# Corner weights by columns on ScalarE in a four-layer convolution network: three buffers, and two pauses in the order

## The chip, the cores and the metric

The kernel runs on one NeuronCore of one Trainium2 chip. A core has five engines with queues of their own, and each executes its queue strictly in order: TensorE (PE in the profile, with its weight loads as PEld), VectorE (DVE), ScalarE (ACT), GpSimd (POOL) and SyncE (SP), which here only starts DMAs. GpSimd starts DMAs too: the indirect gathers. The metric is the device time of one execution in microseconds (us). The kernel before takes 7763.29 us, the median of 8 runs that lie between 7756.68 and 7767.76.

## The reference

The input is four images of 256 channels and 64 x 64 pixels, all in float32. Four layers follow, each `x = x + layer(groupnorm(x))`:

- **Layer 0, deformable convolution.** A 1x1 convolution with batch norm and leaky ReLU gives `y`. A projection of `y` is the picture that is sampled. A 3x3 depthwise convolution of `y` gives, for each pixel, 4 groups and 9 points, an offset and a softmax weight. Each point is sampled bilinearly, so from four corners with four weights, and the 9 points of a group are summed:

```python
return tap(x0, y0, (1 - wx) * (1 - wy)) + tap(x0 + 1, y0, wx * (1 - wy)) \
     + tap(x0, y0 + 1, (1 - wx) * wy) + tap(x0 + 1, y0 + 1, wx * wy)
...
dout = (samp * mr).sum(-1)
```

  Then come an output projection, a squeeze-and-excite scaling by channel means over the whole image, and a feedforward 256 to 1024 to 256.
- **Layer 1, linear attention.** A 1x1 convolution gives q, k, v; a 5x5 depthwise convolution gives a second set; heads of 8 channels compute `vk = v k^T`, `out = vk q / (sum(k) q + eps)`, then a projection.
- **Layer 2, a 3x3 convolution** with binarised weights.
- **Layer 3, attention against pooled keys**: 4096 queries, 1024 keys from a 2x2 max pool, softmax, output convolution.

## The kernel before, in words

**The sampling.** For each image a table in DRAM holds, for each pixel, a row of 256 numbers: the 64 channels of one group at that pixel and its neighbours, so that one gathered row has all four corners of a point. `sample` (from line 557) walks an image in 16 blocks (NBLK) of 18 rounds (BR), 288 rounds in all. In each round `gathered` (L589) starts four indirect gathers from GpSimd's queue, one per group, each of 128 rows into a tile `g` (seven buffers). The row numbers are read from the tile `sl`, which a DMA fills for each block. TensorE then does eight small matmuls (L602): the gathered rows against a matrix `wm` of 128 rows and 16 columns for each corner, which holds the row's corner weight in the column of the pixel that the row belongs to and zero elsewhere. So the matmul weighs the corners and sums the points at once, into `acc`.

**The matrices `wm`.** `weigh` (L582) makes them for three rounds (WR) at a time: an array of 128 x (3 rounds x 16 corners x 16 columns). One VectorE instruction multiplies the table `own` (which column a row belongs to, the same for all) with the 48 weights of the three rounds. There are two buffers. The product for the next three rounds is called in the first round of the present three.

**What follows `acc`.** Each two rounds ScalarE copies `acc` to SBUF (`moved`, L607), TensorE transposes it (`turned`, L612), ScalarE copies the result in two halves into `dT` (`spread`, L622). After a block come the output projection (L635), two additions and a batch norm.

**The other work beside it.** The sampling of image n runs with other images' later layers beside it, all in one order written by the program: `beside` (in `run`) advances the sampling by one round and then each other generator until its spent cost matches its share. The totals that these shares are of are constants: FEED for the feedforward, LINEAR for the linear attention, SECOND for layer 2 and 3 of an image. The first image's convolution runs ahead; then come four stages: image 0's sampling beside the other images' convolutions and offsets; image 1's beside binarising, image 0's feedforward (the first fifth) and linear attention (the rest); images 2 and 3 beside the feedforward and linear attention of the image before and, from 0.2 to 0.9 of the stage, layers 2 and 3 of the one before that. After the last gather the rest of the images' layers run. In these stages TensorE, VectorE, ScalarE and GpSimd execute in the very order in which the program lists the instructions.

**The linear attention's output** (`output`, L911). For half a row block (1024 pixels): `dens` makes the denominators on TensorE (L919), `inverse` adds eps and takes the reciprocal on VectorE (L923, L924), `head` spreads the reciprocals over the channels with TensorE (`rden`, L932), `scaled` multiplies on VectorE (`ot`, L936), `proj` projects (L941), `relu` is ScalarE's (L945). They stand in a list; `staged` lines them up in steps, and each step of the generator takes one from the list. The depthwise 5x5 convolutions (L178, 25 instructions a chunk on VectorE, about 1.3 us each) run between.

**The pooled attention** (`layer3`). For 128 queries at a time: scores (L1185), maximum (L1186), exponential on ScalarE (`pe`, L1191), transposes (L1197), a copy on ScalarE (`pT`, L1199), the values (L1203), the reciprocal of the sum (L1206) and the scaling on ScalarE (`m`, L1208). After four of these the output convolution reads `m` on TensorE (L1212) and the result is added. A `yield` with a cost stands between these pieces, and is where other work is let in.

Of the kernel before, what the change touches and what calls it, by code (L numbers as in the profile page):

```python
# [9 lines left out]
F32 = mybir.dt.float32  # L10
I32 = mybir.dt.int32
AF = mybir.ActivationFunctionType
ALU = mybir.AluOpType
# [4 lines left out]
P = 128  # L18
# [3 lines left out]
NB = HW // 512  # L22
NT = HW // P
G, PT = 4, 9
# [5 lines left out]
RP, WR, UR, BG = 14, 3, 2, 2  # L30
RS, GP = RP * PT, RP * PT + 2
BR, BP, OB = PT * BG, GP * BG, RP + 2
NBLK = HW // BP
# [5 lines left out]

CONVOLVE, OFFSETS, BINARY = NB * 9 + 26, 60, 62  # L40
FEED = NB * 40 + 8
LINEAR, LAST, ASIDE = 930, 592, 9
STEPS = 900
CONV, SECOND = NB * 22.5 + 11, 555
EPS_BN = 1e-5
EPS_GN = 1e-5
EPS_ATT = 1e-5
# [24 lines left out]
class Net:  # L72
# [485 lines left out]
    def sample(self, n, ssum):  # L558

        nc, sp = self.nc, self.sp
        table = self.tab[n].rearrange("g y x s c -> (g y x) (s c)")
        blocks, images, at, dp, dT, po, later = {}, {}, {}, {}, {}, {}, {}

        def halves(name):

            t = self.ps1.tile([P, 2, 256], F32, name=name, tag=name)
            return cycle([t[:, 0], t[:, 1]])  # L570

        accs, dps = halves("acc"), halves("dp")

        def load(b):
            blocks[b] = sl = sp.tile([P, BR, G * 5], F32, name="sl")
            for h in range(BG):
                rows = self.s_d[n][(b * BG + h) * GP * PT:(b * BG + h + 1) * GP * PT]
                to = sl[:, h * PT:(h + 1) * PT]
                nc.sync.dma_start(to[0:RS], rows[0:RS * PT].rearrange("(r p) f -> p r f", p=RS))
                nc.sync.dma_start(to[RS:P], rows[RS * PT:].rearrange("(p r) f -> p r f", r=PT))  # L580

        def weigh(b, r):  # L582

            wm = self.gp.tile([P, WR, 4 * G, OB], F32, name="wm")
            sh = [P, WR, 4 * G, OB]
            nc.vector.tensor_tensor(  # L586
                wm, self.con("own").unsqueeze(1).unsqueeze(1).to_broadcast(sh),
                blocks[b][:, r:r + WR, G:].unsqueeze(3).to_broadcast(sh), ALU.mult)
            return wm  # L589

        def gathered(sl, wm, acc, r):
            r4, acc = r % WR, acc[:, r % UR * P:(r % UR + 1) * P]
            g = self.gp.tile([P, G, 256], F32, name="g", bufs=7)
            for i in range(G):
                nc.gpsimd.indirect_dma_start(  # L595
                    out=g[:, i, :], out_offset=None, in_=table,
                    in_offset=bass.IndirectOffsetOnAxis(ap=sl.bitcast(I32)[:, r, i:i + 1], axis=0))


            for x in range(2):  # L600
                for i in range(G):
                    nc.tensor.matmul(acc[32 * i:32 * i + 32, :], wm[:, r4, 4 * i + 2 * x:4 * i + 2 * x + 2, :],  # L602
                                     g[:, i, x * P:(x + 1) * P], start=x == 0, stop=x == 1)

        def moved(acc, u):
            at[u] = sp.tile([P, UR, P], F32, name="at")
            nc.scalar.copy(at[u].rearrange("p v c -> p (v c)"), acc)  # L607

        def turned(u):
            dp[u] = next(dps).rearrange("p (v g s o) -> p v g s o", v=UR, g=G, s=2)  # L610
            for v in range(UR):
                nc.tensor.transpose(dp[u][:, v].rearrange("p g s o -> p (g s o)"), at[u][:, v], self.ident)  # L612

        def spread(b, r, u):

            if b not in dT:
                dT[b] = sp.tile([P, G, BR, OB], F32, name="dT", bufs=1)
                images[b] = sp.tile([P, KT, BP], F32, name="yb")
                nc.sync.dma_start(images[b], self.y_d[n][:, :, b * BP:(b + 1) * BP])
            for s in range(2):  # L620
                hs = slice(64 * s, 64 * s + 64)
                nc.scalar.copy(dT[b][hs, :, r:r + UR], dp[u][hs, :, :, s, :].rearrange("p v g o -> p g v o"))  # L622

        def shared(b):


            v = dT[b].rearrange("p g (h r) o -> p (g h) o r", r=PT)
            both = sp.tile([P, G * BG, 2], F32, name="both")
            nc.vector.tensor_reduce(both, v[:, :, RP:], AX.X, ALU.add)
            nc.scalar.copy(v[:, :, RP:, 0], both)  # L630

        def project(b, m):
            po[m] = self.ps("po")
            for k in range(G):
                nc.tensor.matmul(po[m][:, 0:BR * OB], self.ow[:, k, m * P:(m + 1) * P], dT[b][:, k].rearrange("p r o -> p (r o)"), start=k == 0, stop=k == G - 1)  # L635

        def add(b, m):
            ym = images[b][:, m].rearrange("p (h q) -> p h q", h=BG)
            pm = po[m][:, 0:BR * OB].rearrange("p (h r o) -> p h r o", h=BG, o=OB)
            y4 = ym[:, :, 0:RS].rearrange("p h (r o) -> p h r o", o=RP)  # L640
            nc.vector.tensor_tensor(y4, pm[:, :, :, 0:RP], y4, ALU.add)
            nc.vector.tensor_tensor(ym[:, :, RS:], pm[:, :, 0, RP:], ym[:, :, RS:], ALU.add)

        def finish(b, m):
            ym = images[b][:, m]
            nc.scalar.activation(ym, ym, AF.Identity, bias=self.sh[:, 4 + m:5 + m],
                                 scale=self.inv[:, 4 + m:5 + m], accum_out=ssum[:, m, b:b + 1])
            if m == KT - 1:
                nc.sync.dma_start(self.x2_d[n][:, :, b * BP:(b + 1) * BP], images[b])

        load(0)
        wm = weigh(0, 0)
        for i in range(NBLK * BR):
            b, r = divmod(i, BR)
            for f in later.pop(i, ()):
                f()
            if r % UR == 0:
                acc = next(accs)
            gathered(blocks[b], wm, acc, r)
            if r == 0 and b + 1 < NBLK:  # L660
                load(b + 1)
            if r % WR == 0 and (r + WR < BR or b + 1 < NBLK):
                nxt = weigh(*divmod(i + WR, BR))
            if r % UR == UR - 1:
                todo = [partial(moved, acc, i), partial(turned, i), partial(spread, b, r + 1 - UR, i)]

                todo = [(i + 1 + j + (j == 2 and r < UR) * (6 - 3), f) for j, f in enumerate(todo)]
                if r == BR - 1:
                    todo += [(i + 3, partial(shared, b))]
                    todo += [(i + 6 + m + j, partial(f, b, m)) for m in range(KT) for j, f in enumerate((project, add, finish))]  # L670
                for j, f in todo:
                    later.setdefault(j, []).append(f)
            if r % WR == WR - 1:
                wm = nxt
            yield 1
        for i in sorted(later):
            for f in later[i]:
                f()
# [73 lines left out]
    def layer1(self, n, st, st2):  # L752
        nc, tc, a = self.nc, self.tc, self.a
        rw = lambda v: v.rearrange("p (r w) -> p r w", w=W)
        fl = lambda v: v.rearrange("p r w -> p (r w)")
        with tc.tile_pool(name=f"la{n}", bufs=1, side="right") as sp, \
# [3 lines left out]
            pw = sp.tile([P, 4, C], F32, name="pw")  # L760
# [3 lines left out]
            nc.vector.tensor_tensor(qb, qb, self.vec("qkv_s", n=6), ALU.mult)  # L764
            nc.vector.tensor_tensor(qb, qb, self.vec("qkv_b", n=6), ALU.add)
            yield 6
            ln = sp.tile([P, 4, P], F32, name="ln")
            ld = sp.tile([P, 4, 2, 32], F32, name="ld")
            nc.vector.memset(ld, 0.0)

# [122 lines left out]

            def summed(t):

                pc = self.ps("comb").rearrange("p (e o) -> p e o", e=2)
                for kind in range(2):
                    j = 2 * kind + t
                    nc.vector.tensor_tensor(ln[:, j], sums[:, t, kind], self.con("bd"), ALU.mult)
                    kk = sp.tile([P, 1], F32, name=f"kk{j}")  # L900
                    nc.vector.tensor_reduce(kk, ks[t][:, kind, 0:(NB, NCH)[kind]], AX.X, ALU.add)
                    for h in range(2):
                        nc.vector.tensor_scalar(ld[:, j, h, 16 * h:16 * h + 16], self.con("oh"), kk, None, ALU.mult)
                for kind in range(2):
                    nc.tensor.matmul(pc[:, kind], ln[:, 2 * kind + t], pw[:, 2 * kind + t], start=True, stop=True)
                    nc.vector.tensor_copy(pw[:, 2 * kind + t], pc[:, kind])

            def output(c, qp, aq):
# [47 lines left out]
                none = ()  # L956
# [2 lines left out]
                    staged([(dens, inverse), none, none] + order + [none, outs[1, 0], outs[1, 1]])  # L959
                else:  # L960
                    joined = lambda *fs: [f() for f in fs]
                    items = [(partial(joined, dens, inverse),)]
                    for h in range(2):
                        items += [(partial(joined, *heads[h, j]),) for j in range(4)]
                        items += [(partial(joined, *outs[h, m][:2]), outs[h, m][2]) for m in range(KT)]
# [134 lines left out]
    def layer3(self, n, st, wide=False):  # L1100
        nc, tc, a = self.nc, self.tc, self.a
        M = HW // 4
        with tc.tile_pool(name=f"na{n}", bufs=1, side="left") as sp, \
# [69 lines left out]
            for b in range(NB):  # L1173
                m2 = bp.tile([P, 512], F32, name="m2")
                for j in range(4):
# [30 lines left out]
                    nc.vector.reciprocal(rden, ps[:, P:P + 1])  # L1206
                    yield 1.5
                    nc.scalar.activation(m2[:, j * P:(j + 1) * P], ps[:, 0:P], AF.Copy, scale=rden)  # L1208
                r = self.block(bp, self.x5_d[n], b, "r5", bufs=1)
                for k in range(KT):  # L1210
                    ps = self.ps()
# [171 lines left out]
```

## Time and profile before

| what | value |
|---|---|
| median of 8 runs | 7763.29 us (7756.68 to 7767.76) |
| the profiled execution: its time, its span | 7755.36 us, 7753.6 us |
| first and last gather start | 132.6 us, 6266.0 us |
| TensorE, VectorE, GpSimd, ScalarE busy | 76%, 66%, 66%, 28% of the span |
| gathers | 4608, mean 976 ns, median 946 ns |
| wm products on VectorE | 384, mean 953 ns |

A group on the page names line, engine, operation, the tile written and those read, how often, then the busy time with the mean of one, and last the idle time of the engine just before these instructions with what ended most of it. "issue" means that the profile shows nothing waited for. A line of the waits has the waiting engine and line, what released it, the total in us, how often, and the longest. A line of the timeline has its start, its length, the engine and the instruction, with the idle time before it in brackets. Engines count as busy while an instruction runs on them; instructions of ScalarE in a row overlap a little.

### The profile page before, as it was taken

To read this page: it belongs to the slowest core of one execution; us is meant where nothing else is said; L and a number is where in the kernel's file an instruction comes from. 1 tells how busy PE (TensorE), PEld (TensorE's weight loads), DVE (VectorE), ACT (ScalarE), POOL (GpSimd) and SP (SyncE) were. 2 spreads that over 40 slices of the span, in tenths; PEclk is the share of its full clock that TensorE was granted. 3 is DMA by queue.
4 is the path that set the end of the run, shared out by engine and by line. 5 is a ranking of instruction groups with operands and counts; after the bars stand their busy time and mean duration, and the time that the engine had idled before them with its cause. 6 is when DMAs were issued, how large, how long until landed. Compare 5 with 4: busy or idle time off the path is not lost. (4 is left out here: it accounts for less than half of the span.)

```text
span 7753.6 us, 94114 instructions
## 1 busy us (share of the span) xinstructions
PE 5927.1 (76%) x35776; PEld 3477.8 (45%) x35776; DVE 5117.7 (66%) x6404; ACT 2170.5 (28%) x4648; POOL 5091.1 (66%) x4894
## 2 busy tenths in 40 slices
PE   5666666579676677889767778987677789967899
PEld 2333333334333333346544433465454435744487
DVE  6555553644788887239888882288888834999523
ACT  1111111212222211222233222222332223666315
POOL 2777777777777777777677667677776621977210
PEclk7676776779777677999888888998888889978899
DMA  6564665555544444555544455465444432211221
GB/s 188 151 179 137 172 173 140 170 176 157 159 125 122 127 139 132 167 152 161 149 138 134 121 153 166 138 166 152 142 133 124 126 123 77 65 49 38 69 80 52
DMA packets 744340, 1031.41 MB, mean 133 GB/s; under 512 B 354128, under 2 KB 459984, under 8 KB 742352
## 3 DMA queue, kind: packets, MB, share of 16 engines
q0 software_dynamic: 221184, 604.27, 27.1%
q1 hardware_dynamic: 522704, 421.10, 18.3%
q8 instruction: 284, 4.65, 0.2%
q14 instruction: 168, 1.38, 0.1%
HBM read 856.39 MB, written 168.61 MB: 132 GB/s over the span
## 5 line engine op out<-in xcount | busy, mean ns | idle before, releaser
L595 POOL DMA_INDIRECT g<-tab,sl x4608 | 4497.7, 976 | 1767.9 <-issue 1270.4
L178 DVE SCALAR_TENSOR_TENSOR agg<-pad,vec,agg 128x1024 f32<-128x1024 f32 x2257 | 2904.8, 1287 | 61.8
L602 PE MATMUL acc<-g,wm 128*32 128x128 f32 x18432 | 1298.8, 324 | 1208.6 <-ACT at L607 683.0
L602 PEld LDWEIGHTS acc<-g,wm 128*32 128x32 f32 x18432 | 636.2, 122 | 1921.9 <-ACT at L607 896.1
L1085 PE MATMUL ps<-xd,w 128*128 128x256 f32 x3072 | 716.4, 385 | 4.0 <-ACT v L828 1.7
L586 DVE TENSOR_TENSOR wm<-con,sl 128x768 f32<-128x768 f32 x384 | 365.9, 953 | 422.6 <-PE acc L602 409.1
L1085 PEld LDWEIGHTS ps<-xd,w 128*128 128x128 f32 x3072 | 578.2, 193 | 105.6 <-issue 26.7
L622 ACT COPY dT<-dp 64x128 f32<-64x128 f32 x1152 | 296.8, 258 | 1124.6 <-PE dp L612 790.7
L734 PE MATMUL ps<-x2f,f 128*128 128x512 f32 x1024 | 479.3, 616 | 4.0 <-ACT f L709 4.0
L820 PE MATMUL ps<-xr,qw 128*128 128x512 f32 x768 | 451.8, 719 | 18.3 <-DVE ot L936 7.7
L744 PE MATMUL ps<-hm,f 128*128 128x512 f32 x1024 | 462.0, 599 | 0.0
L719 DVE SCALAR_TENSOR_TENSOR hm<-ps,vec,lk 128x512 f32<-128x512 f32 x256 | 192.1, 751 | 399.3 <-ACT lk L736 394.3
L200 POOL TENSOR_TENSOR av<-av,m 128x1024 f32<-128x1024 f32 x144 | 344.1, 2389 | 105.5 <-ACT m L196 96.8
L1036 POOL TENSOR_TENSOR xd<-xp 128x640 f32<-128x640 f32 x64 | 79.4, 1270 | 492.7 <-DMA xp<-x 266.4
L607 ACT COPY at<-acc 128x256 f32<-128x256 f32 x576 | 214.3, 372 | 519.4 <-PE acc L602 507.8
L736 ACT ACTIVATE lk<-ps,low 128x512 f32<-128x512 f32 x256 | 175.9, 687 | 595.2 <-PE ps L734 595.2
L635 PE MATMUL po<-dT,ow 128*128 128x288 f32 x1024 | 310.7, 453 | 21.6 <-ACT dT L630 14.8
L1203 PE MATMUL ps<-gt,pT 128*128 128x129 f32 x2048 | 303.8, 308 | 29.4 <-ACT pT L1199 29.0
L1203 PEld LDWEIGHTS ps<-gt,pT 128*128 128x128 f32 x2048 | 287.7, 220 | 74.1 <-ACT pT L1199 42.0
L612 PE MATMUL dp<-ident,at 128*128 128x128 f32 x1152 | 273.3, 325 | 60.0 <-ACT dT L622 47.9
L734 PEld LDWEIGHTS ps<-x2f,f 128*128 128x128 f32 x1024 | 191.2, 194 | 230.6 <-issue 217.8
L874 ACT COPY kt<-pt 128x512 f32<-128x512 f32 x256 | 149.3, 584 | 501.0 <-PE pt L870 500.8
(243 smaller groups left out, 7542.4 us busy)
## 6 DMA issues: line engine op xcount, KB each, us to landing
g<-tab,sl POOLq DMA_INDIRECT x4608
x<-x SPq DMA_DIRECT2D x128, 512.0 KB
xr<-x SPq DMA_DIRECT2D x96, 512.0 KB
tab<-xo SPq DMA_DIRECT2D x192, 128.0 KB
x<-in_x SPq DMA_DIRECT2D x32, 512.0 KB
y<-yc SPq DMA_DIRECT2D x32, 512.0 KB
yb<-y SPq DMA_DIRECT2D x64, 256.0 KB
x<-yb SPq DMA_DIRECT2D x64, 256.0 KB
```

The lines of the kernel that those rows point to most:

```text
L178: nc.vector.scalar_tensor_tensor(to, s, wt, acc, ALU.mult, ALU.add)
L200: nc.gpsimd.tensor_tensor(acc, acc, made[t - 1], ALU.add)
L586: nc.vector.tensor_tensor(wm, self.con("own").unsqueeze(1).unsqueeze(1).to_broadcast(sh), blocks[b][:, r:r + WR, G:].unsqueeze(3).to_broad ...
L595: nc.gpsimd.indirect_dma_start(out=g[:, i, :], out_offset=None, in_=table, in_offset=bass.IndirectOffsetOnAxis(ap=sl.bitcast(I32)[:, r, i: ...
L602: nc.tensor.matmul(acc[32 * i:32 * i + 32, :], wm[:, r4, 4 * i + 2 * x:4 * i + 2 * x + 2, :], g[:, i, x * P:(x + 1) * P], start=x == 0, st ...
L622: nc.scalar.copy(dT[b][hs, :, r:r + UR], dp[u][hs, :, :, s, :].rearrange("p v g o -> p g v o"))
L635: nc.tensor.matmul(po[m][:, 0:BR * OB], self.ow[:, k, m * P:(m + 1) * P], dT[b][:, k].rearrange("p r o -> p (r o)"), start=k == 0, stop=k ...
L734: nc.tensor.matmul(ps, f1[:, k, m * P:(m + 1) * P], x2[:, k], start=k == 0, stop=k == KT - 1)
L744: nc.tensor.matmul(ps, f2[:, k, m * P:(m + 1) * P], hm[:, k], start=k == 0, stop=k == 4 * KT - 1)
L820: nc.tensor.matmul(ps, qw[:, k, m * P:(m + 1) * P], x[:, k], start=k == 0, stop=k == KT - 1)
L1085: nc.tensor.matmul(ps[:, e], w[:, k, t, 2 * half + e, m * P:(m + 1) * P], v[:, 2 * half + e, k, t:t + 8], start=i % 6 == 0, stop=i % 6 == 5)
L1203: nc.tensor.matmul(ps[:, 0:P + 1], pT[:, m], gt[:, m], start=m == 0, stop=m == 7)
```

## The change

`weigh` now returns the tile and a function `columns`, which writes the sixteen columns of `wm` one by one on ScalarE: the 48 weights times one column of `own`, given as the scale of an activation. The tile has three buffers instead of two. The columns of the three rounds after next are written in the second and third round of the present three, eight in each; those of the first six rounds of an image are written at its start. VectorE's product is gone.

Two pauses are added: an empty item behind the reciprocals in the list of the linear attention's output (in the stages with sampling; the last image's list had such items already), and a `yield 1.5` behind the fourth scaling of the pooled attention. The totals LINEAR and SECOND are raised with them. The tile `ln` of the linear attention, four parts kept for an image, becomes a rotating one of two parts.

```diff
-LINEAR, LAST, ASIDE = 930, 592, 9
+LINEAR, LAST, ASIDE = 938, 592, 9
-CONV, SECOND = NB * 22.5 + 11, 555
+CONV, SECOND = NB * 22.5 + 11, 568
...
-            wm = self.gp.tile([P, WR, 4 * G, OB], F32, name="wm")
-            sh = [P, WR, 4 * G, OB]
-            nc.vector.tensor_tensor(
-                wm, self.con("own").unsqueeze(1).unsqueeze(1).to_broadcast(sh),
-                blocks[b][:, r:r + WR, G:].unsqueeze(3).to_broadcast(sh), ALU.mult)
-            return wm
+            wm = self.gp.tile([P, WR, 4 * G, OB], F32, name="wm", bufs=3)
+
+            def columns(o0, o1):
+                for o in range(o0, o1):
+                    nc.scalar.activation(wm[:, :, :, o], blocks[b][:, r:r + WR, G:], AF.Copy, scale=self.con("own")[:, o:o + 1])
+
+            return wm, columns
...
-        wm = weigh(0, 0)
+        weights = [weigh(0, r) for r in range(0, 2 * WR, WR)]
+        for _, columns in weights:
+            columns(0, OB)
...
-            gathered(blocks[b], wm, acc, r)
+            gathered(blocks[b], weights[0][0], acc, r)
             if r == 0 and b + 1 < NBLK:
                 load(b + 1)
-            if r % WR == 0 and (r + WR < BR or b + 1 < NBLK):
-                nxt = weigh(*divmod(i + WR, BR))
+            if r % WR and i - r % WR + 2 * WR < NBLK * BR:
+                if r % WR == 1:
+                    weights.append(weigh(*divmod(i - 1 + 2 * WR, BR)))
+                weights[2][1]((r % WR - 1) * OB // 2, r % WR * OB // 2)
...
-            ln = sp.tile([P, 4, P], F32, name="ln")
...
+                ln = bp.tile([P, 2, P], F32, name="ln", tag="v1")
...
-                    items = [(partial(joined, dens, inverse),)]
+                    items = [(partial(joined, dens, inverse),), none]
...
                     nc.scalar.activation(m2[:, j * P:(j + 1) * P], ps[:, 0:P], AF.Copy, scale=rden)
+                yield 1.5
                 r = self.block(bp, self.x5_d[n], b, "r5", bufs=1)
```

More of the change, by code (lines that the diff above doesn't have):

```diff
@@ L673, in sample @@
             if r % WR == WR - 1:
-                wm = nxt
+                weights.pop(0)
             yield 1
@@ L898, in summed @@
                     j = 2 * kind + t
-                    nc.vector.tensor_tensor(ln[:, j], sums[:, t, kind], self.con("bd"), ALU.mult)
+                    nc.vector.tensor_tensor(ln[:, kind], sums[:, t, kind], self.con("bd"), ALU.mult)
                     kk = sp.tile([P, 1], F32, name=f"kk{j}")
@@ L904, in summed @@
                 for kind in range(2):
-                    nc.tensor.matmul(pc[:, kind], ln[:, 2 * kind + t], pw[:, 2 * kind + t], start=True, stop=True)
+                    nc.tensor.matmul(pc[:, kind], ln[:, kind], pw[:, 2 * kind + t], start=True, stop=True)
                     nc.vector.tensor_copy(pw[:, 2 * kind + t], pc[:, kind])
```

## The prediction

> **What bounds the kernel now.** I read the page's totals first.
>
> ```profile
> span 7753.6 us, 94114 instructions
> ...
> PE 5927.1 (76%) x35776; PEld 3477.8 (45%) x35776; DVE 5117.7 (66%) x6404; ACT 2170.5 (28%) x4648; POOL 5091.1 (66%) x4894
> ```
>
> No engine is full, so the stages must be read one by one. The windows between the first gathers of the four images and the end of the last one (columns: window, length, then busy time of PE, weight loads, DVE, ACT, POOL, granted clock, DMA share):
>
> ```profile
> 132.00:1622.00 1490.00, 963.83 (x6596) 501.20 (x6596) 801.26 (x1115) 253.63 (x693) 1129.93 (x1152) 0.70 0.57 162
> 1623.00:3118.00 1495.00, 1103.32 (x6660) 550.07 (x6661) 1057.35 (x1121) 331.43 (x840) 1128.37 (x1152) 0.77 0.49 142
> 3118.00:4692.00 1574.00, 1249.51 (x8481) 759.54 (x8480) 1140.69 (x1377) 444.27 (x1039) 1118.67 (x1153) 0.89 0.50 147
> 4692.00:6267.00 1575.00, 1251.06 (x8482) 760.62 (x8481) 1140.71 (x1377) 444.38 (x1039) 1119.98 (x1153) 0.89 0.50 144
> ```
>
> 6134 of the 7754 us are gathering, 1152 gathers to a stage. The groups on the page say what a gather costs.
>
> ```profile
> L595 POOL DMA_INDIRECT g<-tab,sl x4608 | 4497.7, 976 | 1767.9 <-issue 1270.4
> ...
> L586 DVE TENSOR_TENSOR wm<-con,sl 128x768 f32<-128x768 f32 x384 | 365.9, 953 | 422.6 <-PE acc L602 409.1
> ```
>
> The mean is 976 ns, the median of the line 946, and 0.30 us passes between two undisturbed gathers: 1.25 us, or 1440 us for 1152. The stages take 1490, 1495, 1574 and 1575 us. So POOL sets the end of each, and there are 374 us over the floor: gathers longer than 946 ns (30 x 4608 = 138 us) and longer pauses before them. The timeline shows what a long gather lies beside.
>
> ```profile
> 3015.69 0.95 POOL L595 DMA_INDIRECT g<-tab,sl  x1 [0.30 <-issue]
> ...
> 3016.44 0.95 DVE L586 TENSOR_TENSOR wm<-con,sl 128x768 f32<-128x768 f32 x1
> 3016.95 1.27 POOL L595 DMA_INDIRECT g<-tab,sl  x1 [0.31 <-issue]
> ...
> 3018.52 0.94 POOL L595 DMA_INDIRECT g<-tab,sl  x1 [0.30 <-DMA g<-tab,sl]
> ```
>
> The gather that starts while VectorE multiplies two SBUF operands takes 1.27 us instead of 0.95. Laid over each other for the whole trace, 354 gathers took over 1.0 us; 234 of them overlap one of the 384 wm products, and hold 104 of the 138 us (28, 27, 25 and 24 by stage). The scalar_tensor_tensor of L178 with one large SBUF operand lies beside many more gathers and leaves them at 0.95.
>
> The pauses come from the waits of POOL in the third stage; the fourth is alike, while the first two have 12.2 and 19.4 us on the second of these lines.
>
> ```profile
> POOL g L595 <- issue: 309.2, 1014, 0.6
> POOL g L595 <- PE acc L602: 121.8, 65, 7.1
> ```
>
> POOL waits for TensorE to free a gather buffer. Without the usual 0.30 us that is 121.8 - 65 x 0.30 = 102 us. Some 19 of them (23.2 us in 13 waits) lie in the feedforward at 3280 to 3510, where TensorE is full:
>
> ```profile
> 3280.00:3510.00 230.00, 209.02 (x1180) 106.22 (x1173) 73.35 (x139) 62.33 (x142) 160.07 (x164) 0.96 0.52 151
> ```
>
> The other 83 lie where both attentions run; from 4350 to 4600 alone 56.1 us in 19 waits, with VectorE busy 214 of 250 us and TensorE 195.
>
> **The change, part by part.** *The product leaves VectorE.* 384 x 953 ns = 366 us of VectorE go, and its waits for TensorE before them (409 us; 32 in the third stage, most in the first two, where VectorE has room). VectorE itself sets no stage, so this is worth what POOL gets of it. First the long gathers: in stages one and two POOL hardly waits, and 28 + 27 us come off; in the other two some of a shorter gather is spent in the next wait, and I take three quarters of 49, 37. Together -92. Bounds 0 and -104.
>
> On this the Trainium skill speaks against the change: "SBUF — State Buffer", Who interferes with whom, says that a product of two SBUF inputs takes only the read half of the port pair shared with GpSimd, and infers that descriptor generation, which writes, isn't held up by it. By that this term would be nothing. The 234 long gathers say otherwise here; the same section also has that a GpSimd instruction that reads SBUF is held up, and this one reads its row numbers there.
>
> *The waits of POOL for TensorE.* In 4350 to 4600, VectorE loses 14 products of 0.953 us and 1.6 us of waits, 15 us. That is 30% of the 50.4 us of stall there (56.1 - 19 x 0.30). The two pauses take away TensorE's waits in that window for the pooled attention's scaled rows (ACT m L1208, 8.9 us) and for the reciprocal (DVE rd L924, 5.6 us): 14.5 us or 29%. What they let pass meanwhile is the next round's work on the same queue. The two overlap, and not each microsecond reaches POOL: I take 45% of 83, 37 us for each of stages three and four, -75. Bounds 0 and -166. The feedforward's 19 us stay, as TensorE is full, and so do the few in the first two stages.
>
> *ScalarE's columns.* 384 x 16 = 6144 activations of 48 elements, in eights, in two of three rounds. The nearest rows with a scale from a column, both operands in SBUF, and one narrow strided copy:
>
> ```profile
> L630 ACT COPY dT<-both 128x16 f32<-128x16 f32 x64 | 13.1, 205 | 223.9 <-DVE both L629 223.9
> L709 ACT ACTIVATE f<-f,ex 128x1024 f32<-128x1024 f32 x8 | 8.7, 1141 | 0.0
> L1133 ACT ACTIVATE gw<-gw,g_r 128x128 f32<-128x128 f32 x8 | 2.9, 393 | 0.2 <-PE ps L1124 0.2
> ```
>
> From 1024 to 128 elements is 0.835 ns an element, so 48 take 393 - 80 x 0.835 = 326 ns. Two of L1213 (807 ns each) end within 1.51 us, so neighbours overlap by 0.10: 0.226 us apart, 1.9 us for eight, 1389 us in all, 347 a stage. The ends are 0.105 apart (the copy of 16 less the overlap; 645 us) and 0.326 (no overlap; 2003 us). I take 0.226, as the same form with the same operands gives it. ScalarE then has 444 + 347 = 791 of 1574 us in stages three and four, from 28% to 50%, and at the upper end 61%: not the bound on its own. The cover is that it waits. In the third stage it waited 145 us for the feedforward's sums, 135 and 105 us for transposes, and the columns, due four rounds later, stand ahead of those waits on its queue. The third buffer was last read by matmuls that the copy of acc before them has waited for already.
>
> What stays is that a copy behind a burst is up to 1.9 us later. TensorE's waits for ScalarE other than the copy of acc were 53 us in the third stage (m 15, pe 15, dT 13, smaller ones 10). Grown with ScalarE's load (x 1.8) they add 43, of which POOL feels about a third to a half, since it stood 102 us while TensorE was idle 324: +20 a stage, +40. Bounds 0 and +86; beyond that it is the rival below.
>
> *Starts.* Each image begins with 32 columns (7.3 us) where one product stood. Seven gather buffers, 7 x 5 us, cover it: 0, or +7 each if the buffers were full. In the built program VectorE now has chunk work ahead of the first image's last coordinates, since no wm product bars its queue: at most 5 x 1.29 + 1.33 + 4 x 0.63 = 10 us before the first gather, and SP issues one 512 KB load earlier. Part is covered by the table's writes: +4, ends 0 and +10.
>
> *The rest.* LINEAR and SECOND only follow the lengthened lists (one more step per output, 1.5 per block). The linear layer's ln in a rotating buffer waits for a free one twice an image: 0. After the last gather the pauses only reorder image 2's attention: 0, within 8 either way; the last image runs alone, where a pause is none.
>
> Sum: -92 - 75 + 40 + 4 = -123. The profiled execution took 7755.4 us (span 7753.6 and 1.8 around it), so 7632. It lies 7.9 under the median of the runs shown, below the lowest of them; on the median I expect 7640.
>
> **Rivals.** *All waits go.* VectorE at 86% in the attention windows speaks for it, the full TensorE in the feedforward against: -104, -166 and some +10 give 7503.
> *The port alone.* TensorE is 79% busy in stages three and four and could keep POOL waiting whatever VectorE does: 7763 - 92 + 44 = 7715.
> *The product does not hold up a gather*, the skill's rule told above; worked out from the rows, the long gathers then stay and come from something beside the products: 7763 - 75 + 44 = 7732. The line 0.95, 1.27, 0.94 is against it.
> *Slower: ScalarE's bursts on TensorE's path.* A round in the attentions goes from TensorE to ScalarE and back (pe, pT, kt, at) within 5 us; a burst ahead of one of them holds TensorE and so the buffers. Stages three and four have 2 x 192 bursts of 1.9 us. Without the +40 the change gains 163, so it turns at 163 / 384 = 0.42 us of a burst on the path. At 0.6 us it gives 7763 - 163 + 230 = 7830. For it: ScalarE is often blocked in order (m waits 68 us for VectorE in the third stage) and then catches up with nearly twice the work. Against: it is idle 72% of that stage.
>
> **How the numbers follow.** Forecast 0.40, its own spread 7570 to 7690; all waits 0.12; port alone 0.23; no port 0.07; slower 0.15; an even balance 0.03. 0.2% is 16 us, about what a measurement of this kernel can tell from no change. The two small gains can shrink into that, so faster 0.80, same 0.05, slower 0.15. The range from 7500 takes in nearly all of the first rival and ends at 7770, where the slower case begins; about 0.18 is left out.
>
> **What would show it.** Right: wm on ScalarE x6144 near 326 ns; ScalarE busy near 3560 us, VectorE near 4750; the gather's mean near 953; stages near 1462, 1468, and 1538 twice; POOL's waits for acc from 277 to about 200. The port step is wrong if the mean stays at 976, the second if stages three and four stay above 1550 with short gathers. The forecast fails if TensorE's waits for pe, pT, kt and dT grow by more than they lose.

## The result and the profile after

The changed kernel takes 7736.64 us (median of 11 runs, 7730.67 to 7740.28) against 7761.06 for the kernel before in the runs taken with it: a ratio of 0.9969, 95% interval 0.9961 to 0.9976. It is 24 us or 0.31% faster; 123 us were forecast, and the range began at 7500 and ended at 7770. So the sign and the range held, and the size was five times too large. The profiled execution took 7733.04 us, with a span of 7731.3.

The windows between the first gathers of the images (columns as before: window, length, busy time of PE, PEld, DVE, ACT, POOL, clock, DMA share, GB/s):

```profile
138.00:1604.00 1466.00, 955.47 (x6598) 498.48 (x6598) 715.77 (x1025) 606.48 (x2262) 1108.78 (x1152) 0.70 0.57 164
1604.00:3072.00 1468.00, 1091.44 (x6667) 547.64 (x6668) 966.86 (x1009) 674.66 (x2342) 1101.10 (x1152) 0.78 0.49 145
3072.00:4655.00 1583.00, 1253.97 (x8480) 760.23 (x8478) 1059.07 (x1281) 792.71 (x2575) 1097.84 (x1152) 0.89 0.50 146
4655.00:6239.00 1584.00, 1257.58 (x8493) 762.14 (x8481) 1059.80 (x1282) 792.88 (x2575) 1098.69 (x1152) 0.89 0.49 143
```

The first two stages came down from 1490 and 1495 us to 1466 and 1468, as forecast (1462 and 1468). The third and fourth were to fall to 1538 and rose from 1574 and 1575 to 1583 and 1584. The groups on the page and, below them, the waits of POOL in the third stage:

```profile
L596 POOL DMA_INDIRECT g<-tab,sl x4608 | 4406.4, 956 | 1831.3 <-issue 1266.7
...
L588 ACT ACTIVATE wm<-sl,con 128x48 f32<-128x48 f32 x6144 | 1487.0, 364 | 24.8 <-DMA sl<-sd 11.7
```

```profile
POOL g L596 <- issue: 305.0, 1000, 0.6
POOL g L596 <- PE acc L603: 159.6, 84, 6.6
```

The gather's mean fell from 976 to 956 ns, which is 20 x 4608 = 92 us. That is the size of the port term, though not by its working: a mean of 953 ns or 104 us was looked for, of which 92 were to reach the stages. But POOL's waits for TensorE in the third stage, less the usual 0.30 us of each, rose from 102 to 159.6 - 84 x 0.30 = 134 us, where they were to fall to 65 or, with ScalarE's price, 85. The first gather starts at 138.3 us instead of 132.6, and what follows the last gather takes 1492 us instead of 1487. Together: -24 - 28 + 9 + 10 + 6 + 5 = -22, the difference of the spans.

What TensorE waited for in the third stage, in the kernel before:

```profile
PE acc L602 <- ACT at L607: 189.1, 86, 12.1
PE ps L1212 <- ACT m L1208: 14.9, 6, 5.8
PE pt L1197 <- ACT pe L1191: 14.9, 11, 4.3
...
PE rden L932 <- DVE rd L924: 6.0, 3, 4.3
```

and in the changed kernel:

```profile
PE acc L603 <- ACT at L608: 211.9, 89, 8.4
PE pt L1202 <- ACT pe L1196: 20.8, 10, 10.1
...
PE ps L1218 <- ACT m L1213: 2.5, 3, 1.1
...
PE rden L937 <- DVE rd L929: 0.8, 1, 0.8
```

The two pauses did what they are made for: the waits for the scaled rows (14.9 to 2.5 us) and for the reciprocal (6.0 to 0.8) are all but gone. Others have grown: that for the copy of `acc` by 23 us and that for `pe` by 6. VectorE is busy 1059 of 1583 us instead of 1141 of 1574, so in this stage what was taken off it became idle time.

Three theories are tested: (A) ScalarE's bursts cost TensorE the time and the pauses helped; (B) TensorE's order sets the pace and neither the relief nor the pauses matter; (C) the pauses cost the time. "The pauses" are here always the two pauses with the totals LINEAR and SECOND raised for them; the last experiments take pause and total apart.

### The profile page after: what moved, and what is told of

Same layout as the page of the kernel before. It is cut to its first block, busy times and chain, and to the rows that moved or that the text cites. A ratio compares the mean times of both kernels' runs of the same rounds, so it can differ in the third digit from the quotient of the medians.

```text
span 7731.3 us, 99783 instructions
## 1 busy us (share of the span) xinstructions
PE 5931.7 (77%) x35776; PEld 3478.7 (45%) x35776; DVE 4783.8 (62%) x6020; ACT 3563.4 (46%) x10792; POOL 4999.4 (65%) x4894
## 4 chain that ended last, share of the span: by engine, by line
PE 38%; DVE 17%; POOL 8%; issue 6%; ACT 6%; DMA 3%; SPq 0%; POOLq 0%; DVEq 0%; ACTq 0%
DVE agg L178 12%; POOL g L596 7%; PE ps L739 6%; PE ps L749 6%; PE ps L1090 4%; PE acc L603 4%; PE ps L824 3%; PE ps L1208 3%; PE s L1190 2%; PE ps L946 2%; DMA g<-tab,sl 2%; PE po L636 2%; DVE mx L1191 1%; POOL av L200 1%; PE pt L1202 1%
## 5 line engine op out<-in xcount | busy, mean ns | idle before, releaser
L596 POOL DMA_INDIRECT g<-tab,sl x4608 | 4406.4, 956 | 1831.3 <-issue 1266.7
L588 ACT ACTIVATE wm<-sl,con 128x48 f32<-128x48 f32 x6144 | 1487.0, 364 | 24.8 <-DMA sl<-sd 11.7
L1190 PE MATMUL s<-ph,th 128*128 128x512 f32 x512 | 278.7, 657 | 27.2 <-DVE ot L941 9.3
```

Source lines behind the costliest of these rows:

```text
L588: nc.scalar.activation(wm[:, :, :, o], blocks[b][:, r:r + WR, G:], AF.Copy, scale=self.con("own")[:, o:o + 1])
L596: nc.gpsimd.indirect_dma_start(out=g[:, i, :], out_offset=None, in_=table, in_offset=bass.IndirectOffsetOnAxis(ap=sl.bitcast(I32)[:, r, i: ...
L1190: nc.tensor.matmul(s[i], tv[:, 4 * b + j], ph[:, i * 512:(i + 1) * 512], start=True, stop=True)
```

## The experiments

The lengths of the stages below are from the first gather of an image to the end of its last.

| kernel | third and fourth stage, us | gather's mean, ns | whole, us (ratio to before, 95%) |
|---|---|---|---|
| before | 1574, 1574 | 976 | 7763 |
| changed | 1583, 1584 | 956 | 7737 (0.9961 to 0.9976) |
| columns, no pauses | 1555, 1554 | 956 | 7669 (0.9873 to 0.9903) |
| VectorE's product, both pauses | 1611, 1611 | 977 | 7842 (1.0093 to 1.0123) |
| neither product nor columns, both pauses | 1581, 1577 | 957 | 7723 (0.9940 to 0.9971) |
| columns for images 0 and 1, product for 2 and 3, no pauses | 1572, 1568 | 964 | 7697 (0.9908 to 0.9936) |
| columns, pooled attention's pause | 1570, 1569 | 955 | 7713 (0.9933 to 0.9960) |
| columns, linear attention's pause | 1549, 1549 | 955 | 7655 (0.9853 to 0.9884) |
| neither product nor columns, no pauses | 1559, 1554 | 955 | 7665 (0.9864 to 0.9894) |
| each column written twice, no pauses | 1758, 1761 | 955 | 8142 (1.0479 to 1.0511) |

### Without the pauses

```diff
-LINEAR, LAST, ASIDE = 938, 592, 9
+LINEAR, LAST, ASIDE = 930, 592, 9
-CONV, SECOND = NB * 22.5 + 11, 568
+CONV, SECOND = NB * 22.5 + 11, 555
-                    items = [(partial(joined, dens, inverse),), none]
+                    items = [(partial(joined, dens, inverse),)]
-                yield 1.5
                 r = self.block(bp, self.x5_d[n], b, "r5", bufs=1)
```

> The columns on ScalarE alone: both pauses out and the two totals back at 930 and 555, everything else as in the changed kernel. Three theories on why the third and fourth stage (images 2 and 3 gathered) went from 1574 to 1583 us instead of to 1538. (A) ScalarE's bursts of eight columns lie on TensorE's path and cost 30 us and more a stage, and the pauses gave back what they could: then this run's third and fourth stage are longer than 1583, near 1595. (B) TensorE's order paces these stages, so the shorter gathers only wait longer and VectorE's relief is worth nothing; the pauses matter little: within 5 us of 1583. (C) The pauses themselves cost the time, by making the lists longer: the stages fall to 1560 or less. The first stage, which has neither pause, stays at 1466 by all three.

It took 7669.48 us, ratio 0.9888 (0.9873 to 0.9903). The windows of its third and fourth stage:

```profile
3069.00:4625.00 1556.00, 1253.11 (x8482) 765.34 (x8481) 1059.44 (x1281) 793.53 (x2575) 1097.79 (x1153) 0.89 0.50 148
4625.00:6180.00 1555.00, 1249.30 (x8481) 763.21 (x8480) 1059.73 (x1281) 793.05 (x2575) 1097.09 (x1152) 0.89 0.49 146
```

The busy times are those of the changed kernel within 1%; the stages are 28 us shorter. Theory C holds and A falls, and so does B in what it says of the pauses: a gain of 87 us was there, and the pauses gave 64 us of it back by the profiled executions (67 by the medians). POOL's waits in this third stage:

```profile
POOL g L596 <- PE acc L603: 125.5, 68, 7.4
```

That is 125.5 - 68 x 0.30 = 105 us, against 102 before and 134 with the pauses. The same kernel on another chip later:

> The same kernel as the run without pauses (columns on ScalarE, 930 and 555). Two chips have now taken 13% longer for every kernel, also for the one before, and the four runs with a changed pace were made on these. If this run lands on such a chip too, its ratio to the kernel before is what those four are to be read against: by theory S (only a pause costs) it equals that of SECOND 568, SECOND 549 and LINEAR 938 without a pause (0.997, 1.001 to 1.002, 0.997), which already differ from each other by 0.5% and so speak for theory F. If it lands on a chip as at first, it is 0.989 again, third and fourth stage 1555.

7672.03 us, ratio 0.9881 (0.9864 to 0.9897), stages 1557 and 1554. The first result stands. In the fourth stage each of the 16 blocks, from first gather to first gather, takes the same time as on the first chip within 0.1 us (in the third, 14 of 16 within 0.2). Against these, the changed kernel's excess of 30 us there isn't spread evenly: its ninth block is 7.5 us longer and its fourteenth 9.0, its thirteenth 6.5 shorter. So the waits repeat with the written order, and a changed order moves them by several microseconds a block both ways.

### The pauses alone

```diff
-LINEAR, LAST, ASIDE = 930, 592, 9
+LINEAR, LAST, ASIDE = 938, 592, 9
-CONV, SECOND = NB * 22.5 + 11, 555
+CONV, SECOND = NB * 22.5 + 11, 568
-                    items = [(partial(joined, dens, inverse),)]
+                    items = [(partial(joined, dens, inverse),), none]
+                yield 1.5
                 r = self.block(bp, self.x5_d[n], b, "r5", bufs=1)
```

> The kernel before with the two pauses and the totals 938 and 568 alone; VectorE still makes the matrices. By (A) the pauses help by what TensorE waited for the scaled rows and the reciprocal: third and fourth stage from 1574 to some 1555, the whole 30 to 40 us faster. By (B) they move little: within 5 us of 1574, the whole within 10 us. By (C) they cost: 1580 or more, the whole 15 us slower or more. The gather's mean stays at 976 ns by all three.

7841.86 us, ratio 1.0108 (1.0093 to 1.0123): 85 us slower, with VectorE making the matrices as before. The third stage:

```profile
3122.00:4733.00 1611.00, 1258.91 (x8480) 760.91 (x8480) 1139.93 (x1377) 442.47 (x1040) 1122.47 (x1153) 0.88 0.49 143
```

The waits of POOL there are as many microseconds as in the changed kernel:

```profile
POOL g L595 <- PE acc L602: 159.6, 73, 7.1
```

So the pauses cost 28 us a stage with the columns and 37 without them. That is theory C again, and it doesn't need ScalarE's columns.

### Nobody builds the matrices

```diff
-            if r % WR and i - r % WR + 2 * WR < NBLK * BR:
-                if r % WR == 1:
-                    weights.append(weigh(*divmod(i - 1 + 2 * WR, BR)))
-                weights[2][1]((r % WR - 1) * OB // 2, r % WR * OB // 2)
...
-            if r % WR == WR - 1:
-                weights.pop(0)
```

> The changed kernel with the matrices of the first three rounds of an image used for all its rounds, so that neither ScalarE nor VectorE builds any others; the corner weights of all other rounds are left out of the result. This shows what taking the product from VectorE is worth when nobody pays for it. By (A) the third and fourth stage fall far below 1574, to 1520 or less, and the difference to 1583 is the price of the columns. By (B) they stay above 1555: TensorE keeps POOL waiting over 100 us a stage though nothing builds matrices. First and second stage near 1466 by both.

7722.88 us with both pauses, 14 us under the changed kernel (11 by the ratios); third and fourth stage 1581 and 1577. Theory A, which wanted 1520 or less, falls here too; B's number, above 1555, came. The same edit without the pauses:

> No pauses, and the matrices of the first rounds of an image used for all its rounds, so that no engine builds any others; the corner weights of the other rounds are left out of the result. If ScalarE's columns cost the third and fourth stage next to nothing, they stay within 5 us of 1555; if ScalarE's bursts had a price of 20 us a stage, as the prediction took it, they fall to 1535.

7665.35 us, ratio 0.9879. The third stage:

```profile
3073.00:4632.00 1559.00, 1256.60 (x8481) 766.39 (x8480) 1059.38 (x1281) 451.06 (x1071) 1096.55 (x1152) 0.89 0.50 148
```

ScalarE is at 451 us instead of 793, and the stage is no shorter than with the columns (1559 and 1554 against 1555 and 1554). The columns cost these stages nothing that can be measured. This run also bounds what VectorE's relief is worth: here its product is gone and no one pays for it, and POOL's waits for TensorE are

```profile
POOL g L596 <- PE acc L603: 127.6, 60, 9.5
```

so 110 us less the usual pauses, not fewer than the 102 before. The relief can hide in this number, since a shorter gather can also mean a longer wait. The stages of the two kernels without product and pauses are 15 to 20 us shorter than before, and their gathers together 21 to 24 us. If the prediction's quarter of that is lost in waits, the relief gave at most 3 us a stage; if nothing is lost, it gave nothing. With both pauses the stages fell by 30 and 34 us when the product went (1611 and 1611 to 1581 and 1577), 6 and 12 us more than their gathers. So the relief is worth something in one order and about nothing in another.

### Columns for two images only

```diff
...
+            if n >= 2:
+                sh = [P, WR, 4 * G, OB]
+                nc.vector.tensor_tensor(
+                    wm, self.con("own").unsqueeze(1).unsqueeze(1).to_broadcast(sh),
+                    blocks[b][:, r:r + WR, G:].unsqueeze(3).to_broadcast(sh), ALU.mult)
...
-            if r % WR and i - r % WR + 2 * WR < NBLK * BR:
+            if n >= 2:
+                if r % WR == 0 and (r + WR < BR or b + 1 < NBLK):
+                    weights.append(weigh(*divmod(i + WR, BR)))
+            elif r % WR and i - r % WR + 2 * WR < NBLK * BR:
...
```

> Columns on ScalarE for images 0 and 1, VectorE's product for images 2 and 3, no pauses. If the gain is that of shorter gathers where POOL alone sets the pace, the first two stages are those of the changed kernel (1466 and 1468) and the last two those of the kernel before (1574): about 7755 - 52 + 6 at the start, near 7710, faster than both. If the loss in the last two stages comes from elsewhere (the pauses, the third buffer, the new place of ln), they stay at 1583 and the time is near 7735.

7696.76 us, ratio 0.9922 (0.9908 to 0.9936); stages 1466, 1469, 1572 and 1568. The gather's mean is 964 ns, between 956 and 976, as half of the products are there. The last two stages are within 6 us of the kernel before, so neither the third buffer nor the new place of `ln` is what lengthened them. It loses 27 us to the kernel with columns for all images: the columns pay in the full stages too, once the pauses are out.

### Each column twice

```diff
...
-                for o in range(o0, o1):
+                for o in [o for o in range(o0, o1) for _ in range(2)]:
...
```

> No pauses, each column written twice on ScalarE (the same values, so the result stays): 6144 more activations, 347 us more of ScalarE a stage, 73% of stage three. If the columns hide in ScalarE's waits, the stages stay within 10 us of 1555 and the time near 7680. If a burst lies on TensorE's path, the second burst costs as much as the first or more: by the prediction's 20 us a stage, 1575 and more.

8141.73 us, 5% slower. The second of a pair writes the same place as the first and does not overlap it: it starts 0.39 us after the first, where neighbours of the changed kernel start 0.225 apart; the next pair follows after 0.24. Sixteen take 5.21 us in the timeline of this kernel, eight take 1.95 in that of the changed kernel:

```profile
4003.11 5.21 ACT L588 ACTIVATE wm<-sl,con 128x48 f32<-128x48 f32 x16
```

```profile
4015.16 1.95 ACT L588 ACTIVATE wm<-sl,con 128x48 f32<-128x48 f32 x8
```

So the load rose by more than was meant (12288 columns and 3792 us), and the first three stages read

```profile
139.00:1633.00 1494.00, 897.76 (x6588) 481.93 (x6591) 704.37 (x1008) 1170.49 (x3799) 1108.61 (x1152) 0.70 0.56 161
1633.00:3135.00 1502.00, 997.26 (x6682) 516.63 (x6672) 975.09 (x1027) 1228.40 (x3876) 1100.33 (x1152) 0.76 0.48 141
3135.00:4894.00 1759.00, 1311.29 (x8441) 796.32 (x8439) 1060.82 (x1279) 1350.37 (x4108) 1096.18 (x1153) 0.86 0.44 131
```

In the third ScalarE is busy 77%, and it is 204 us longer than with each column once. The price of a burst isn't constant: 342 us of columns a stage cost nothing, 557 us more cost 204. The slower rival was a real mechanism, but in such a stage it begins somewhere between 50% and 77% of ScalarE; no run lies between. ScalarE's share alone doesn't set the price: in the first two stages it is busy 78% and 82%, and they are only 31 and 36 us longer (1494 and 1502).

### Which pause

The pooled attention's pause alone, with SECOND at 568:

> Columns on ScalarE with the pooled attention's pause alone (and SECOND 568). Without pauses the third and fourth stage took 1555 and 1554 us and what follows the last gather 1487; with both 1583, 1584 and 1492. Theory P: it is this pause, since it makes one more step in each of the blocks 6 to 14, where the waits for a gather buffer grew (blocks 8 and 9 from 2 and 4 us to 9 each): stages near 1580, the whole near 7730. Theory L: it is the linear attention's pause: stages here stay near 1555, the whole near 7672.

7713.2 us; stages three and four 1570 and 1569, and 1495 us behind the last gather. And the linear attention's alone, with LINEAR at 938:

> Columns on ScalarE with the linear attention's pause alone (and LINEAR 938). Theory P: stages three and four stay near 1555, the whole near 7670. Theory L: they are near 1580, the whole near 7725. The second stage, which has this pause and no pooled attention, stays at 1467 by both. If each run shows half of the 28 us, the two pauses add up and the cause is the longer lists as such.

7654.7 us, ratio 0.9868 (0.9853 to 0.9884), the fastest kernel of the study; stages 1549 and 1549. So the pooled pause costs 15 us a stage, the linear one gains 6, and both together cost 28, each with its raised total. Neither theory held: they don't add up. In the third stage of the run with the pooled pause TensorE's waits show the exchange that the changed kernel has too:

```profile
PE acc L603 <- ACT at L608: 197.2, 84, 9.9
PE pt L1202 <- ACT pe L1196: 19.2, 11, 5.6
...
PE ps L1218 <- ACT m L1213: 1.5, 3, 0.9
```

Without any pause these were

```profile
PE acc L603 <- ACT at L608: 177.4, 86, 10.3
...
PE pt L1202 <- ACT pe L1196: 12.2, 11, 2.0
...
PE ps L1217 <- ACT m L1213: 7.3, 7, 2.2
```

The pause takes 6 us off the wait for `m` and puts 7 on that for `pe` and 20 on that for the copy of `acc`.

### Pause or pace

Each pause was made together with a raised total, which sets how fast that work is advanced against the rounds. Two theories: (S) a pause costs as such; (F) what costs is which pieces of the two attentions fall into one round. Four kernels should tell: SECOND at 568 or 549 without a pause, the pooled pause with SECOND left at 555, and LINEAR at 938 without a pause. The edits are against the kernel without pauses.

```diff
-CONV, SECOND = NB * 22.5 + 11, 555
+CONV, SECOND = NB * 22.5 + 11, 568
```

> Columns on ScalarE, no pause at all, only SECOND at 568 instead of 555: the same instructions with the convolution and pooled attention of the other image advanced 2% faster. What is open is why the pooled attention's pause costs 15 us in each of stages three and four, the linear one gains 6, and both together cost 28 and not 9. Theory S (the pause as such: each lengthens the pooled attention's chain): here the stages stay within 4 us of 1555. Theory F (the fit: what costs is which pieces of the two attentions fall into the same round, and any shift of them changes that): they move by 5 to 25 us, either way, though nothing waits longer by itself.

```diff
-CONV, SECOND = NB * 22.5 + 11, 555
+CONV, SECOND = NB * 22.5 + 11, 549
```

> As before with SECOND at 549, so that the other image's work is advanced 1% slower and 6.7 of its cost is left to the end of its window. Theory S: within 4 us of 1555. Theory F: another value, 5 to 25 us off in either direction.

```diff
                     nc.scalar.activation(m2[:, j * P:(j + 1) * P], ps[:, 0:P], AF.Copy, scale=rden)
+                yield 1.5
```

> The pooled attention's pause with SECOND left at 555: until the first pause everything falls into the same rounds as without it. Theory S: third and fourth stage near 1570, as with the pause and 568. Theory F: a value of its own, off 1570 by 5 us or more; if it comes to 1555, the pause itself costs nothing and the 15 us were all from the changed pace.

```diff
-LINEAR, LAST, ASIDE = 930, 592, 9
+LINEAR, LAST, ASIDE = 938, 592, 9
```

> No pauses, only LINEAR at 938 instead of 930: the linear attention advanced 0.9% faster. Theory S: within 4 us of 1555, and the 6 us gained with the linear pause are that pause's. Theory F: it moves too, and may reach the 1549 of that run without any pause.

These runs can't be set beside the others: on their chip every kernel, the one before too (8788 us), took 13% longer, with GpSimd standing between gathers in all four stages for a cause that the profile only calls remote, as it shows no instruction that ended the wait:

```profile
POOL g L596 <- remote: 678.1, 327, 6.0
POOL g L596 <- PE acc L603: 601.0, 212, 30.0
```

The second set of the same kernels met the same trouble on another chip.

> No pause, SECOND at 568, on a chip where the kernel before takes its usual time (on the last one every kernel was 13% slower, GpSimd standing between gathers in all stages, so that the stages tell nothing). Theory S (the pause as such costs): third and fourth stage within 4 us of 1555, the whole near 7670. Theory F (the fit of the two attentions' pieces to the rounds): 5 to 25 us off 1555 in either direction.

> No pause, SECOND at 549. Theory S: within 4 us of 1555. Theory F: another value, 5 to 25 us off; on the slow chip this one was the slowest of the four, so above 1565.

> The pooled attention's pause, SECOND at 555. Theory S: near 1570, as with the pause and 568 (1570 and 1569). Theory F: off that by 5 us or more; at 1555 the pause itself would cost nothing. On the slow chip this was the fastest of the four, which speaks for F.

> No pauses, LINEAR at 938. Theory S: within 4 us of 1555, so the 6 us that the linear pause gained are its own. Theory F: a value of its own.

> No pause, SECOND at 568; without pauses and at 555 the third and fourth stage took 1555 to 1558 and 1554 us, with the pause and 568 1570 and 1569. Theory S (the pause costs): within 4 us of 1555, the whole near 7671. Theory F (the changed fit costs): 5 us and more off 1555; at 1565 to 1575 the whole cost of the pooled attention's pause is that of the pace set for it, and the whole is near 7700.

So did the last run, SECOND at 568 once more (8762.72 against 8785.07 us). Within these conditions the kernels can be compared with each other by their ratios to the kernel before:

| kernel, columns on ScalarE | ratio, first chip | ratio, later chips |
|---|---|---|
| no pause, SECOND 568 | 0.9971 (0.9959 to 0.9983) | 0.9968 (0.9952 to 0.9983), 0.9975 (0.9959 to 0.9991) |
| no pause, SECOND 549 | 1.0009 (0.9994 to 1.0024) | 1.0017 (1.0003 to 1.0031) |
| pooled pause, SECOND 555 | 0.9946 (0.9931 to 0.9961) | 0.9942 (0.9925 to 0.9959) |
| no pause, LINEAR 938 | 0.9969 (0.9953 to 0.9984) | 0.9967 (0.9952 to 0.9982) |

There the pace alone, without any pause, moves the time: 549 is 0.4 to 0.5% slower than 568, some 35 to 40 us. In the traces the third and fourth stage take 1820 us each at 549 in both runs, 1803 to 1817 at 568 in its three, and 1787 to 1795 with the pause at the old total, which is the fastest of the four kernels. So the pace moves these stages by itself. By S the pace is free and the kernel with the pause would be the slowest; that fails there. Whether the pause costs anything against no pause at 555 isn't known there. This speaks for F. On the chips with the usual times, on which the 28 us were measured, pause and pace have not been parted, and the kernel without pauses was not timed in the disturbed conditions; so F is supported, not shown, for the result itself.

## Why the prediction was right in sign and wrong in size

That the sign held is owed to the port term, which came. That the time fell into the range is partly luck: of the other two large terms one came out 139 us above its forecast and one 40 below, so that they partly cancel; the first alone would have led to some 7780, outside the range.

**The port: right.** -92 forecast; without pauses the four stages are 94 us shorter, and the whole is 87 us faster by its span, as the first gather comes later. The exact agreement is luck: the gathers' mean fell by 20 ns x 4608 = 92 us and not by the 104 looked for, but nearly all of it came in the third and fourth stage too, where I had taken three quarters. 1574 to 1555 is 19 of the 21 us that the shorter gathers are there, and a share of that may be VectorE's relief. The section Who interferes with whom of the Trainium skill's "SBUF — State Buffer" infers that a product of two SBUF inputs does not hold up descriptor generation. In these runs 977 and 976 ns with the product, 964 with half of them and 955 to 957 without any speak against that for gathers that read their row numbers from SBUF. The rival built on it fell.

**POOL's waits for TensorE: wrong, and the step that failed.** "I take 45% of 83, 37 us for each of stages three and four, -75" had two halves, and neither held; by the prediction's own sign the step is wrong, as stages three and four stayed above 1550 us with short gathers. VectorE's relief, 15 us of a 50 us stall, was worth next to nothing: with its product gone and no pauses the waits are 105 us, with nobody building matrices 110, before 102, and what it can have given besides is at most 3 us a stage, or 6 and 12 in the order with both pauses. VectorE at 86% of a window looked like the pace-setter, but of the 36 us that it was idle there it waited 19 for TensorE's values and scores (12.6 and 6.5). What it no longer does became idle time, 433 us in the third stage before and 497 without pauses. The pauses were costed at +29% of the stall won, from the waits that they remove. They removed them, and the stage got longer: waits for `pe`, `dT` and the copy of `acc` rose by more, the last from 177 to 212 us, a wait that the prediction had set aside. The effect of the pauses with their totals is +64 us over the whole profiled execution (7731.3 against 7666.9), 57 of it in stages three and four. So the step comes to about +64 instead of -75. I had looked up what ends with a pause and not what then falls into the next round. Why the later pieces fall so badly, by the pause or by the raised total, stays open.

**ScalarE's columns: mis-sized.** +40 forecast; 0 measured, as the runs with and without columns agree without pauses (1555 and 1554 against 1559 and 1554), and with pauses differ by 2 and 7 us a stage. The price of the instructions was right: 0.226 us apart forecast; eight in 1.95 us and 1487 us in all were measured, against 1.9 and 1389. The single duration is 364 ns and not 326. That they hide in ScalarE's waits, as argued, fits this. The growth of TensorE's waits in proportion to ScalarE's load was the wrong rule: no price at half the stage, 204 us at 77%. (At the prediction's upper end ScalarE would have had 945 of 1574 us, 60% and not 61.)

**Starts and the rest.** The first gather came 5.7 us later, where +4 was forecast; what follows the last gather took 5 us more, within the "0, within 8 either way"; without pauses it is as before (1487).

**The rivals.** "The port alone" at 7715 is what the columns without pauses come nearest to in kind, but as ScalarE's price was none they reach 7669. "Slower: ScalarE's bursts" did not happen at this load and did at the doubled one. "All waits go" failed: the waits grew. No rival had the pauses as a loss; I gave them only a gain.

## What to carry to other kernels

Where engines run in a written order and none is full, price an added pause from both sides: it removes the wait that it was put behind, and it moves every later piece against the other work; only a run without it says which is larger. Test a change of several parts with one part out before the whole is judged: here the columns were worth 1.1%, and the pauses hid three quarters of that. Relief of an engine that waits within its busy windows is worth only what the engine that sets the pace gets from it, here the shorter gathers.

## What was not expected of the hardware

- Of the 104 us that gathers beside VectorE's products took too long, 92 came back when the products went, 20 ns on the mean of 4608, also in the stages where POOL waits over 100 us for TensorE.
- Neighbouring activations that write different columns start 0.225 us apart though each takes 0.364; of two that write the same column the second starts 0.39 us after the first (5.21 us for sixteen).
- ScalarE's share in the third and fourth stage could rise from 28% to 50% at no measurable cost, and at 77% they were 13% longer; in the second stage 82% made it 2% longer.
